# Row 0 of a two-layer graph kernel, loaded as two halves of 512 columns instead of pairs of whole blocks

## The chip, the cores and the metric

The kernel runs on one NeuronCore of one Trainium2 chip. A core has five engines that work side by side, each with its own queue of instructions: TensorE (PE in the profile; its weight loads are shown as PEld) multiplies matrices into PSUM, VectorE (DVE) and ScalarE (ACT) work element by element, GpSimd (POOL) does small things here, and SyncE (SP) issues the loads and stores, which 16 DMA engines carry out. An engine takes its instructions in the order in which the program wrote them; semaphores make it wait for another engine or for a load. The metric is the device time of one execution in microseconds (us).

## The reference

Inputs are x (4096 nodes x 64 features), a 4096 x 4096 matrix adj of float32 that is mostly zeros, and small weights. Cut to what matters:

```python
h = relu(layernorm(x))
x1 = tanh(concat([adj @ h, h]) @ W[0])        # hop 0
x2 = tanh(concat([adj @ x1, x1]) @ W[1])      # hop 1
x = x + x2
h = relu(layernorm(x))
support = h @ weight
mask = adj != 0
rank = cumsum(mask, axis=1); deg = rank[:, -1:]
k = minimum(deg, 100); pos = rank - (deg - k)
w = mask * where(pos > 0, 0.5 ** (k - pos), 0)
out = x + w @ support + bias
```

So adj is needed as numbers twice, since hop 1 cannot start before hop 0 has given x1, and once as counts: the weight of an entry depends on how many nonzero entries follow it in its row.

## The kernel before

**Tiling.** adj is taken transposed, in blocks of 128 source nodes (on the partitions, the axis that a matmul sums over) by 1024 destination nodes. There are four rows of destinations (I = 0 to 3) and 32 blocks in each (b = 0 to 31); a block is 512 KB. A chunk of eight blocks has the same 1024 nodes as a row, so blocks 0 to 7 are row 0's own nodes. The matrix is 64 MB and doesn't fit into SBUF.

**Two sweeps.** sweep1 (L418) reads all of adj once, in units of two blocks (1 MB), 16 a row, from block 31 down to block 0. Each unit gets hop 0 on TensorE (agg_pair, L266: two matmuls of 64 output rows, one for each half of 512 columns, side by side in the two column groups of the array) and count_pair (L248) on VectorE: nonzero entries are marked (L254, or for some units on ScalarE, mark_on_act, L240), the mark and the running count are stored as one byte an entry in `code` (L261), and the count goes on (L262). Where x1 of a block is known already (b < 8 I), hop 0 and hop 1 are done in one matmul of 128 rows (L483). sweep2 (L811) loads again the blocks for which hop 1 is missing (72, by its plan at L816, row 0's blocks 8 to 31 last), does their hop 1 and, between these, layer 1 with weights that ScalarE and VectorE make out of `code` (L690, L682, L685); its order is planned by a cost model when the program is built (clock, use, decode).

**What sets the order in sweep1.** The loop over units (L447) writes the instructions of all engines, unit by unit: loads up to k + 5 (load, L426), norms, counting, matmuls, then one step of whatever generator stands in `steps`. A loaded unit goes into a place (places, L106): five of a ring, or parts of `code` that are not yet written. A place is free when its former unit has been counted and multiplied; SP waits for that when it issues the load, and all later loads stand behind it.

**The norms.** ln_relu (L184) takes up to eight blocks in three steps (sum and centre, sum of squares, scale), with ScalarE squaring (L193) and GpSimd taking the power (L197). Before unit 0, VectorE norms blocks 30 and 31, then 24 to 29, then 16 to 23; the chunks 8 to 15 and 0 to 7 follow at units 2 and 5. features_T (L285) transposes a chunk on TensorE, own_share (L227) multiplies it with W.

**The end of row 0.** When row 0 is summed, finish_row(0) (L350) runs as steps between the first units of row 1: the sums go to SBUF (L364), x1 is made (L210, L223), transposed and multiplied with W[1] (L336) and copied out (L348). Then hop 1 of row 0's own eight blocks is done from the last four units of row 0, which are held in their places until then:

```python
            own = [v for k in sorted(held) for v in held[k]]
            for n, (b, a) in enumerate(own):
                agg_pair(acc[0][:, 0, :], at(b)[:, D:], a, n == 0, n == len(own) - 1)
            held.clear()
```

After it L390 adds its product, totals (L298) and count_after (L303) turn the row's counts into what follows each entry, and set_after (L310) stores that; settle (L408) later subtracts it from `code`.

Of the kernel before, what the change touches and what calls it, by code (L numbers as in the profile page):

```python
# [44 lines left out]
def gnn_kernel(  # L45
# [61 lines left out]
    for J in range(NCH):  # L107
        for j in range(NB // CB):
            v = code[J][j].rearrange("p b i -> p (b i)").bitcast(F32)
            v = v.rearrange("p (s i) -> p s i", i=CW)  # L110
            places.append([v, J * NB // 2 + (NB - CB * (j + 1)) // 2, -1])

    cnts = [cnt[:, i].rearrange("p h i -> p (h i)") for i in range(2)]
# [35 lines left out]
    def load_weights():  # L149
        nc.sync.dma_start(wb, weights)  # L150
        for h in range(2):
            rows = slice(h * D, (h + 1) * D)
            nc.gpsimd.tensor_copy(
                wz[rows, h], wb[rows, : HOPS * 2].rearrange("p (k a) e -> p k a e", a=2)
            )
        nc.gpsimd.tensor_copy(xw[:D, 1, :], wb[:D, 3, :])
        nc.gpsimd.tensor_copy(xw[D:, 1, :], wb[D:, 2, :])
# [48 lines left out]
    def paired(po, terms, first=True, last=True):  # L206

        for n, (w, v) in enumerate(terms):
            for c in range(NC):
                nc.tensor.matmul(  # L210
                    po[c * D : (c + 1) * D, :], w(c), v(c),
                    start=first and n == 0, stop=last and n == len(terms) - 1,
                )

    def x1_of(po, I, terms, xs, at_=None):


        paired(po, terms, at_ is not None)
        if at_ is not None:
            nc.vector.tensor_tensor(at_, po, flat(pre1[:, chunk(I), :]), op=ALU.add)  # L220
            po = at_
        for c in range(NC):
            nc.scalar.activation(xs[c][:D], po[c * D : (c + 1) * D, :], AF.Tanh)  # L223

    own0 = []

    def own_share(I):  # L227

        h = flat(pre1[:, chunk(I), :])
        po = two(name="po") if I else one(name="po")  # L230
        paired(po, [(lambda c: wz[:, c, 0, 1], lambda c: h)], last=I > 0)
        if I:
            nc.scalar.copy(h, po)
        else:
            own0.append(po)
# [3 lines left out]

    def mark_on_act(I, b, a):  # L240


        m = codes_at(I, b)
        sign = m.bitcast(I8)
        nc.scalar.activation(sign, a, AF.Sign)  # L245
        nc.scalar.activation(m, sign, AF.Square, scale=float((FLAG - 1 + 0.25) ** 0.5))  # L246

    def count_pair(I, b, a, marked):  # L248

        cnt = cnts[I % 2]  # L250
        q = codes_at(I, b)
        m = q if marked else mbuf[:, b // 2 % 2]
        if not marked:
            nc.vector.tensor_scalar(  # L254
                m, a, 0.0, float(FLAG - 1), op0=ALU.not_equal, op1=ALU.mult
            )
        q, m = (v.rearrange("p h i -> p (h i)").bitcast(U16) for v in (q, m))
        if b == NB - 1:
            nc.vector.tensor_scalar(q, m, float(FULL * 257), None, op0=ALU.add)
        else:  # L260
            nc.vector.tensor_tensor(q, m, cnt, op=ALU.add)  # L261
        nc.vector.tensor_scalar(cnt, q, 0x7F7F, None, op0=ALU.bitwise_and)  # L262

# [39 lines left out]
    def count_after(I, tot, acc):  # L303

        banks = [acc[0][:, c, :] for c in range(NC)] if I else [acc[1], acc[0][:, 1, :]]
# [20 lines left out]

    def x1_and_share(I, xs):
# [3 lines left out]
        K_ = P if I else D  # L331
        for h, pt in enumerate(banks):
            pt = pt.rearrange("p (t w c e) -> p t w c e", t=2, w=2, c=NC)
            for t in range(2):
                for c in range(NC):
                    nc.tensor.matmul(  # L336
                        pt[:, t, :, c, :], by_t(xs[c])[:K_, h, t, :], xw[:K_],
# [4 lines left out]
    def halves_of(banks, w):  # L342
        for h, pt in enumerate(banks):
            yield h, pt.rearrange("p (t w c e) -> p t w c e", t=2, w=2, c=NC)[:, :, w]

    def take(dst, banks, w):
        for h, pt in halves_of(banks, w):
            nc.scalar.copy(as_nodes(dst)[:, 2 * h : 2 * h + 2], pt)  # L348

    def finish_row(I, acc, held):  # L350
        if I:

            T = [tmp(name="T") for _ in range(NC)]
            for c in range(NC):
                nc.scalar.copy(T[c][:D], acc[0][:D, c, :])
                nc.scalar.copy(T[c][D:], acc[1][c * D : (c + 1) * D])
            xs = [tmp(name="x1T") for _ in range(NC)]
            for c in range(NC):
                nc.scalar.copy(xs[c][D:], acc[0][D:, c, :])
            terms = [(lambda c: w0, lambda c: T[c])]  # L360
        else:
            xs = [tmp(name="x1T") for _ in range(NC)]
            S = tmp(name="S")
            nc.scalar.copy(S, acc[1])  # L364
            terms = [(lambda c: wz[:, c, 0, 0], lambda c: S)]
        both = tmp([P, CW], U8, name="both")
        yield
        x1_of(one(name="po") if I else own0.pop(), I, terms, xs, T[1] if I else None)
# [3 lines left out]
        if I:  # L372
            yield
        banks = x1_and_share(I, xs)
        counts = count_after(I, tot, acc)
        take(hxs[I][:, :, D:], banks, 0)
        if I == 0:
            yield

            own = [v for k in sorted(held) for v in held[k]]  # L380
            for n, (b, a) in enumerate(own):
                agg_pair(acc[0][:, 0, :], at(b)[:, D:], a, n == 0, n == len(own) - 1)
            held.clear()
            G = tmp(name="G")
            nc.scalar.copy(G, acc[0][:, 0, :])
            yield
            g = by_t(G)
            for h, pt in halves_of(banks, 1):
                for t in range(2):
                    nc.tensor.matmul(  # L390
                        pt[:, t], g[:, h, t, :], wz[:, :, 1, 0, :],
                        start=False, stop=True, skip_group_check=True,
                    )
# [23 lines left out]

    def sweep1():  # L418
        b0 = NB - 2
        load_x(NCH - 1)  # L420
        first = ln_relu(hxs[-1][:, CB - 2 :, :D], pre1[:, b0:, :])
        pairs = [(I, b) for I in range(NCH) for b in range(NB - 1, 0, -2)]
        tiles = []
        held = {}

        def load(upto, done):  # L426

            while len(tiles) < min(upto, len(pairs)):
                k = len(tiles)
                I, b = pairs[k]  # L430
                free = [v for v in places if k + MARGIN <= v[1] and v[2] < done and v[2] not in held]
                if not free:
                    assert k > done
                    return
                place = min(free, key=lambda v: v[2])
                place[2] = k
                a = place[0]
                n = NB - 1 - b
# [8 lines left out]
        for k, (I, b) in enumerate(pairs):  # L447
            n = k % (NB // 2)
            if n == 0:
                acc = sums_of("acc")  # L450
            if k == 0:
                load(1, 0)
                load_x(2)
                load(2, 0)
                load_x(1)
                load(3, 0)
                load_x(0)
            if k == 6:
                load_weights()
            load(k + 5, k)  # L460
            if k == 0:
                next(first)
                next(first)
                rest = ln_relu(hxs[-1][:, : CB - 2, :D], pre1[:, NB - CB : b0, :])
                next(rest)
                for _ in first:
                    pass
                next(rest)
                more = ln_relu(hxs[2][:, :, :D], pre1[:, chunk(2), :])
                for _ in rest:  # L470
                    pass
                next(more)
                steps.append(more)
            if k in (2, 5):
                q = 1 - k // 3
                steps.append(ln_relu(hxs[q][:, :, :D], pre1[:, chunk(q), :]))
            a = tiles[k]
            count_pair(I, b, a, k in marked)
            for r in (1, 0):
# [9 lines left out]
                if I == 0 and g < CB:  # L489
                    held.setdefault(k, []).append((g, a[:, r]))  # L490
            step()
            if k in (4, 6, 9, 13):
                features_T({4: 3, 6: 2, 9: 1, 13: 0}[k])
            if k in (10, 12, 14, 15):
                own_share({10: 3, 12: 2, 14: 1, 15: 0}[k])

            j = k + (2 if k < NB // 2 - 2 else 3)
            if j < len(tiles):
                m = j % (NB // 2)
                if m % 2 == 1 and m >= 3 if j < NB // 2 else m % 3 == 2 and m > 3:  # L500
                    mark_on_act(*pairs[j], tiles[j])
                    marked.add(j)
            if I > 1 and n % 2 == 1:
                settle()
            if n == NB // 2 - 1 and I < NCH - 1:
                steps.append(finish_row(I, acc, held))
# [5 lines left out]

# [7 lines left out]
    def finish_last(acc):  # L520
# [13 lines left out]
        x1_of(one(name="po"), I, [(lambda c: w0, lambda c: T[c])], xs, T[1])  # L534
# [3 lines left out]
        counts = count_after(I, tot, acc)  # L538
# [272 lines left out]
    def sweep2(acc):  # L811
# [14 lines left out]
        def load(k, r, a, t):  # L826
            I, b = blocks[len(tiles)]
            nc.sync.dma_start(a, adjA[I, NB - 2 - b // 2 * 2 + b % 2])
# [132 lines left out]
```

## Time and profile before

| what | us |
|---|---|
| median of three runs | 348.49 (347.23 to 349.1) |
| the profiled execution | 349.98 |
| its span, first to last instruction | 347.3 |
| TensorE busy | 328.1 (94%) |
| VectorE busy | 274.0 (79%) |
| ScalarE busy | 199.9 (58%) |
| read from HBM | 107.15 MB, 312 GB/s over the span |

The profile's times count from the first instruction. A line of the chain of waits has a start, a length and what was late; a line of the timeline has start, length, engine, source line, operation, the tiles written and read, and in brackets how long the engine had been idle and what ended that. A matmul in float32 of 512 columns shows as two records, and the records of the two column groups overlap, so a block of hop 0 is four records. The row numbers L... are lines of the kernel before.

### The profile page before, as it was taken

To read this page: it belongs to the slowest core of one execution; us is meant where nothing else is said; L and a number is where in the kernel's file an instruction comes from. 1 tells how busy PE (TensorE), PEld (TensorE's weight loads), DVE (VectorE), ACT (ScalarE), POOL (GpSimd) and SP (SyncE) were. 2 spreads that over 40 slices of the span, in tenths; PEclk is the share of its full clock that TensorE was granted. 3 is DMA by queue.
4 is the path that set the end of the run, shared out by engine and by line. 5 is a ranking of instruction groups with operands and counts; after the bars stand their busy time and mean duration, and the time that the engine had idled before them with its cause. 6 is when DMAs were issued, how large, how long until landed. Compare 5 with 4: busy or idle time off the path is not lost.

```text
span 347.3 us, 3829 instructions
## 1 busy us (share of the span) xinstructions
PE 328.1 (94%) x1356; PEld 154.7 (45%) x1360; DVE 274.0 (79%) x402; ACT 199.9 (58%) x204; POOL 24.6 (7%) x22
## 2 busy tenths in 40 slices
PE   2787899999999999999999999999999999998995
PEld 0133344333434344344444343243444656467785
DVE  4988688779749999999999585878256799989953
ACT  2087885184447453266043344136458989979980
POOL 2320200000000000000000000412003000003000
PEclk9999999999999999999999999999999999999999
DMA  7999999999999999884989799999998937400012
GB/s 241 413 410 406 410 408 408 411 408 408 411 408 408 406 366 390 286 321 143 416 291 346 287 401 380 355 413 410 408 408 304 356 112 249 166 0 0 3 44 76
DMA packets 30466, 108.44 MB, mean 312 GB/s; under 512 B 2416, under 2 KB 3824, under 8 KB 30448
## 3 DMA queue, kind: packets, MB, share of 16 engines
q1 hardware_dynamic: 30448, 108.21, 81.0%
q8 instruction: 10, 0.16, 0.2%
q14 instruction: 8, 0.07, 0.0%
HBM read 107.15 MB, written 1.05 MB: 312 GB/s over the span
## 4 chain that ended last, share of the span: by engine, by line
PE 73%; DMA 18%; ACT 3%; issue 2%; DVE 2%; SPq 1%; ACTq 0%; DVEq 0%
PE acc L483 24%; PE acc L268 17%; PE accl L750 12%; PE acc_low L268 12%; DMA codes<-in_adjA_dram 11%; DMA ring<-in_adjA_dram 7%; PE pt L336 2%; PE pto L798 2%; ACT weights L690 2%; PE po L210 2%; PE py L577 1%; DVE weights L685 1%; ACT codes L245 1%; DVE bits L682 0%; PE pt L390 0%
## 5 line engine op out<-in xcount | busy, mean ns | idle before, releaser
L690 ACT ACTIVATE weights<-codes 128x1024 fp32r<-128x1024 uint8 x90 | 86.7, 1044 | 12.7 <-PE accl L750 9.8
L483 PE MATMUL acc<-ring,hx 128*128 128x512 f32 x176 | 76.5, 594 | 0.0
L268 PE MATMUL acc<-ring,hx 128*64 128x512 f32 x288 | 66.9, 599 | 0.8 <-DMA ring<-in_adjA_dram 0.7
L750 PE MATMUL accl<-weights,feat 128*128 128x512 f32 x254 | 63.5, 400 | 1.3 <-DVE feat L624 1.0
L750 PEld LDWEIGHTS accl<-weights,feat 128*128 128x128 f32 x254 | 46.0, 188 | 21.2 <-ACT weights L690 7.3
L483 PEld LDWEIGHTS acc<-ring,hx 128*128 128x128 f32 x176 | 33.2, 190 | 43.1 <-issue 43.1
L268 PE MATMUL acc_low<-codes,hx 128*64 128x512 f32 x192 | 45.7, 595 | 3.6 <-DMA codes<-in_adjA_dram 3.4
L268 PE MATMUL acc_low<-ring,hx 128*64 128x512 f32 x128 | 34.7, 660 | 9.3 <-DVE hx L200 6.3
L412 DVE TENSOR_TENSOR codes<-codes,after 128x2048 uint16<-128x2048 uint16 x32 | 38.3, 1220 | 0.1
L268 PEld LDWEIGHTS acc<-ring,hx 128*64 128x64 f32 x288 | 19.2, 136 | 40.0 <-issue 31.9
L246 ACT ACTIVATE codes<-codes 128x2048 uint8<-128x2048 int8 x19 | 36.3, 1910 | 0.6
L254 DVE TENSOR_SCALAR mbuf<-ring 128x2048 uint8<-128x2048 f32 x30 | 36.6, 1220 | 0.0
L245 ACT ACTIVATE codes<-ring 128x2048 int8<-128x2048 f32 x8 | 15.3, 1914 | 30.1 <-DMA ring<-in_adjA_dram 26.3
L685 DVE TENSOR_SCALAR weights<-bits 128x1024 fp32r<-128x1024 f32 x37 | 26.6, 719 | 7.1 <-PE accl L750 3.7
L261 DVE TENSOR_TENSOR codes<-mbuf,cnt 128x1024 uint16<-128x1024 uint16 x41 | 28.4, 692 | 1.5
L262 DVE TENSOR_SCALAR cnt<-codes 128x1024 uint16<-128x1024 uint16 x64 | 27.5, 429 | 2.2
L268 PEld LDWEIGHTS acc_low<-codes,hx 128*64 128x64 f32 x192 | 14.2, 136 | 29.2 <-issue 20.3
L245 ACT ACTIVATE codes<-codes 128x2048 int8<-128x2048 f32 x11 | 21.0, 1913 | 10.0 <-DMA codes<-in_adjA_dram 10.0
L682 DVE TENSOR_SCALAR bits<-codes 128x1024 uint32<-128x1024 uint8 x37 | 25.6, 691 | 0.8
L598 POOL TENSOR_TENSOR pre<-pre,wb 128x512 f32<-128x512 f32 x4 | 5.5, 1379 | 262.9 <-DVE xc L192 262.9
L268 PEld LDWEIGHTS acc_low<-ring,hx 128*64 128x64 f32 x128 | 9.6, 148 | 29.8 <-issue 13.9
L261 DVE TENSOR_TENSOR codes<-codes,cnt 128x1024 uint16<-128x1024 uint16 x19 | 13.1, 690 | 8.4 <-ACT codes L246 7.6
(89 smaller groups left out, 239.0 us busy)
## 6 DMA issues: line engine op xcount, KB each, us to landing
ring<-in_adjA_dram SPq DMA_DIRECT2D x74, 512.0 KB, 6.6
ring<-in_adjA_dram SPq DMA_DIRECT2D x37, 1024.0 KB, 8.4
codes<-in_adjA_dram SPq DMA_DIRECT2D x26, 1024.0 KB, 18.2
pre<-in_x_dram SPq DMA_DIRECT2D x4, 256.0 KB, 7.5
xres<-in_x_dram SPq DMA_DIRECT2D x4, 256.0 KB, 6.6
out_dram<-o SPq DMA_DIRECT2D x3, 256.0 KB, 2.6
out_dram<-o SPq DMA_DIRECT2D x2, 128.0 KB, 2.2
wb<-in_weights_dram SPq DMA_DIRECT2D x1, 192.0 KB, 17.5
```

Source lines behind the costliest of these rows:

```text
L245: nc.scalar.activation(sign, a, AF.Sign)
L246: nc.scalar.activation(m, sign, AF.Square, scale=float((FLAG - 1 + 0.25) ** 0.5))
L254: nc.vector.tensor_scalar(m, a, 0.0, float(FLAG - 1), op0=ALU.not_equal, op1=ALU.mult)
L261: nc.vector.tensor_tensor(q, m, cnt, op=ALU.add)
L262: nc.vector.tensor_scalar(cnt, q, 0x7F7F, None, op0=ALU.bitwise_and)
L268: nc.tensor.matmul(acc[c * D : (c + 1) * D, :], src, a[:, c * C : (c + 1) * C], start=first, stop=last,)
L412: nc.vector.tensor_tensor(q, q, a[:, None, :].to_broadcast([P, 4, CW // 2]), op=ALU.subtract)
L483: nc.tensor.matmul(acc[0][:, c, :], at(g), a[:, r, c * C : (c + 1) * C], start=g == CB * I - 1, stop=g == 0,)
L682: nc.vector.tensor_scalar(state["bits"], q, float(ZERO), ONE, op0=ALU.subtract, op1=ALU.mult)
L685: nc.vector.tensor_scalar(w, state["bits"].bitcast(F32), 2.0 ** (127 - LOW), None, op0=ALU.mult)
L690: nc.scalar.activation(w, q, AF.Exp, scale=LN2, bias=BIAS)
L750: nc.tensor.matmul(sums[g][:, c, :], feats[J][:, k, :], w[:, c * C : (c + 1) * C], start=first, stop=last,)
```

## The change

Row 0 alone is treated in another way; rows 1 to 3 and sweep2 keep their loops.

- A unit of row 0 is now four blocks by 512 columns, again 1 MB: first the eight units of columns 0 to 511 (blocks 31 down to 0), then those of columns 512 to 1023, of which the unit with blocks 0 to 3 is loaded first. The host lays row 0 out for this, so that a unit is as contiguous as before. The even and the odd block of a pair go to the two column groups of TensorE and are added by the next matmul. sweep2 fetches a block of row 0 as two runs of 2 KB a partition where it was one of 4 KB.
- When the first half is summed (unit 7), x1 of its 512 nodes, which are blocks 0 to 3, is made in steps beside the second half, and hop 1 of these four blocks follows at units 10 to 13, one block at a time. The second half's x1 and hop 1 of blocks 4 to 7 come between the first units of row 1. Units 6, 7, 8 and 15 stay in their places until hop 1 has read them.
- Counting follows the blocks from the end, so it runs in half-size steps (two blocks by 512 columns each), starts two units late, and counts unit 8 last, after unit 15. The units that ScalarE marks in row 0 are 3, 5, 7, 11, 13, 15 (before, 9 as well).
- The first norm takes four blocks, the next four, and the chunk 16 to 23 is split in two; all norms are written by unit 2. Loads are issued up to k + 6; the weights are loaded at unit 1 instead of 6, and the copies made of them are spread over units 1, 4 and 5.
- The parts of `code` of chunk 0 are no longer among the places.

The diff, cut to its core:

```diff
-    for J in range(NCH):
+    for J in range(1, NCH):
...
+    def marks_at(I, b):
         if I:
+            return codes_at(I, b)
+        c, q = b
+        return code[0][q // 2][:, q % 2 * 4 : q % 2 * 4 + 4, c * C : (c + 1) * C]
...
+    def count_step(q, m, cnt, first):
+        q, m = q.bitcast(U16), m.bitcast(U16)
+        if first:
             nc.vector.tensor_scalar(q, m, float(FULL * 257), None, op0=ALU.add)
         else:
             nc.vector.tensor_tensor(q, m, cnt, op=ALU.add)
         nc.vector.tensor_scalar(cnt, q, 0x7F7F, None, op0=ALU.bitwise_and)
...
+        c, n = b
+        for r in (2, 0):
+            count_step(
+                q[:, r : r + 2], m[:, r : r + 2], cnt[:, 0, :, c * (C // 2) : (c + 1) * (C // 2)],
+                n == NB // 4 - 1 and r == 2,
+            )
...
+    def finish_first(acc, quads):
+
+        low, G, po, banks = acc
+        xs = {}
+
+        def x1_half(c):
+            S = tmp(name="S")
+            nc.scalar.copy(S, low[c])
+            yield
+            nc.tensor.matmul(po[c * D : (c + 1) * D], w0, S, start=False, stop=True)
+            xs[c] = tmp(name="x1T")
+            nc.scalar.activation(xs[c][:D], po[c * D : (c + 1) * D], AF.Tanh)
+            yield
+            for h in range(2):
+                pt = nodes(banks[h])
+                for t in range(2):
+                    nc.tensor.matmul(
+                        pt[:, t, :, c, :], by_t(xs[c])[:D, h, t, :], xw[:D],
+                        start=t == 0 and c == 0, stop=True, skip_group_check=True,
+                    )
+            for h in range(2):
+                nc.scalar.copy(
+                    as_nodes(hxs[0][:, :, D:])[:, 2 * h : 2 * h + 2, c], nodes(banks[h])[:, :, 0, c]
+                )
+
+        def hop1(b):
             for c in range(NC):
+                nc.tensor.matmul(
+                    G[c * D : (c + 1) * D, :], at(b)[:, D:], part_of(quads[c, b // 4], b),
+                    start=b == 3, stop=b == 4,
+                )
+
+        yield from x1_half(0)
+        for b in range(3, -1, -1):
+            yield
+            hop1(b)
+        busy.difference_update(k for k in (7, 8))
+        yield "next"
         both = tmp([P, CW], U8, name="both")
+        yield from x1_half(1)
+        yield
+        for b in range(7, 3, -1):
+            hop1(b)
+        busy.difference_update((6, 15))
...
+        marks0 = {1: 3, 3: 5, 7: 7, 9: 11, 11: 13, 13: 15}
+        to_count = [*range(8), *range(9, 16), 8]
+
+        for k in range(2 * NQ):
+            _, (c, q) = units[k]
...
+            if k == 1:
+                copies = load_weights()
+            if k in (1, 4, 5):
+                next(copies, None)
+            load(k + 6)
...
+                for g in (first, first, rest, first, rest, ends[0], rest, ends[0], ends[1], ends[0], ends[1]):
+                    next(g, None)
+                lns[2] = ends[1]
+            a = tiles[k]
+            if c == 0 or q < 2:
+                quads[c, q] = a
+            for b in (4 * q + n for n in (2, 3, 0, 1)):
+                h = b % 2
+                nc.tensor.matmul(
+                    low0[c][h * D : (h + 1) * D, :], at(b)[:, :D], part_of(a, b),
+                    start=b >= NB - 2 if c == 0 else k == 8 and b > 1,
+                    stop=b < 2 if c == 0 else k == 15 and b < 6,
+                )
+            order_ = {
+                0: (1, 1, 2), 1: (0, 1, 0), 2: ("n", 0),
+            }.get(k, ("n", "n") if k == 7 else ("n",))
...
+            if k == 7:
+                own_share(0, po0)
+                steps.append(finish_first((low0, sums0[:, 0, :], po0, banks0), quads))
+            if k >= 7 and steps:
+                if next(steps[0]) == "next":
+                    state0.append(steps.pop(0))
+            if k in (1, 4, 5, 6):
+                features_T({1: 3, 4: 2, 5: 1, 6: 0}[k])
+            if k in (7, 8, 10):
+                own_share({7: 3, 8: 2, 10: 1}[k])
+            if k in marks0:
+                mark(marks0[k])
...
-            nc.sync.dma_start(a, adjA[I, NB - 2 - b // 2 * 2 + b % 2])
+            if I:
+                nc.sync.dma_start(a, adjA[I, NB - 2 - b // 2 * 2 + b % 2])
+            else:
+                v = adjA[0].rearrange("(c j) p (h i) -> j h p c i", c=NC, h=2)[b // 2, b % 2]
+                nc.sync.dma_start(a.rearrange("p (c i) -> p c i", c=NC), v)
```

## The prediction

> **What bounds the kernel now.** I read the page first, then the chain of waits, then one table by stage, and last the timeline of the places where the chain changes hands. The page's own summary of the chain says that TensorE is late most of the time and DMA second:
>
> ```profile
> PE 73%; DMA 18%; ACT 3%; issue 2%; DVE 2%; SPq 1%; ACTq 0%; DVEq 0%
> ```
>
> The chain in order of time (start, length, what) tells where each of the two is late:
>
> ```profile
> 11.78 19.38 DMA codes<-in_adjA_dram
> ...
> 31.17 18.26 DMA codes<-in_adjA_dram
> ...
> 54.32 1.08 PE po L210 x4
> ...
> 61.60 6.87 PE acc L268 x32
> ...
> 71.33 13.88 PE acc_low L268 x64
> 85.21 13.93 PE acc L483 x32
> ```
>
> Row 0 is a stream of loads up to 49.4 us; from 54.3 on it is TensorE without a break up to 218 us. The 6.87 us are hop 1 of row 0's eight own blocks (32 records, 0.86 us a block): the work of which the change moves half. The 13.88 us are eight units (0.435 x 4 = 1.735 us each); L483 is the fused part of row 1. The table by stage (us, then busy PE, PEld, DVE, ACT, POOL, clock, DMA share, GB/s) shows that two resources are full at once:
>
> ```profile
> 6.30:49.40 43.10, 36.93 (x196) 13.23 (x196) 34.08 (x55) 27.90 (x22) 9.25 (x8) 1.00 1.02 408
> 49.40:85.10 35.70, 35.38 (x173) 13.22 (x170) 29.04 (x43) 20.14 (x18) 0.00 (x0) 1.00 1.03 409
> 85.10:99.10 14.00, 14.00 (x36) 6.03 (x34) 10.64 (x16) 3.82 (x2) 0.00 (x0) 1.00 1.03 411
> 99.10:197.80 98.70, 98.41 (x301) 42.55 (x304) 89.50 (x119) 45.21 (x44) 0.00 (x0) 1.00 0.89 338
> ```
>
> In row 0 TensorE has some 6 us idle, so work moved there can hide. But in row 1 the DMA engines run at 409 to 411 GB/s as well. How far TensorE lags behind the loads there is the number that decides. ScalarE shows it, because it marks unit 27 and unit 30 as soon as they land (the bracket: it sat idle until a load came), beside TensorE's first fused weights (unit 28):
>
> ```profile
> 80.59 1.91 ACT L245 ACTIVATE codes<-codes 128x2048 int8<-128x2048 f32 x1 [3.39 <-DMA codes<-in_adjA_dram]
> 85.14 0.30 PEld L483 LDWEIGHTS acc<-ring,hx 128*128 128x128 f32 x2 [0.81 <-issue]
> 88.27 1.91 ACT L245 ACTIVATE codes<-ring 128x2048 int8<-128x2048 f32 x1 [3.83 <-DMA ring<-in_adjA_dram]
> ```
>
> A unit lands every (88.27 - 80.59) / 3 = 2.56 us, so unit 28 lands at 83.15 and TensorE takes it up at 85.14: **a lead of 2.0 us**. It is the smallest of the row (units 29 and 30: 2.9 and 3.9, since fused units cost 3.48 us). TensorE may gain as much as it likes before unit 28; only 2.0 us can pass it.
>
> **The change part by part.**
>
> *TensorE, row 0.* Hop 0 keeps its count: 4 matmuls a unit, still alternating between the two column halves, 1.735 us. From the landing of unit 7 (27.7 in the trace, + 0.5 since the 192 KB of weights now go ahead of it: 28.2) TensorE must do units 7 to 15 (9 x 1.735 = 15.6), four own_share (4 x 0.86 = 3.4), x1 of one half (one matmul alone, 0.43 to 0.86, I take 0.86; half of the 2.08 of L336, 1.04) and hop 1 of four blocks (3.44). ScalarE adds a wait: the tanh of the first half stands behind the marking of unit 7 (about 3.85 us from 32.5), so the transposes start near 37.1 instead of 36.7: 0.4. Sum 24.8 us, so unit 15 is done at 53.0, against 51.4 before. The idle time took most of it, and TensorE is some 2.0 us behind unit 15's landing.
>
> *TensorE, row 1 up to unit 28.* From 49.46 (unit 15's landing): lag 2.0; units 15 to 27 13 x 1.735 = 22.6; x1 of the second half 0.86 + 1.04; hop 1 of the other four blocks 3.44; L390 1.14; counts 0.5; and 0.4 of waiting for the totals (below). Sum 32.0: TensorE is ready at 81.4 for a unit that lands at 83.15. The saving so far is 3.7 us; 2.0 pass, and 1.7 turn into waits for loads at units 25 to 28. I take 1.9, because the first weights after such a wait are not overlapped (0.1).
>
> *After unit 28* nothing absorbs it that I can find. Unit 40 lands at 113.8 and is taken up at 117.35: a lead of 3.5, 1.6 are left. From 121 us the loads are issued as places come free, so they move with the engines. VectorE is near full in rows 2 and 3 but is released by TensorE (5.02 us idle before L220 at 102.70, 0.73 at 148.58). The loads of hop 1 after 184 us wait for TensorE (69.3 us of SP's waits are L828 on it), so the DMA-bound 218 to 237 us move too. Places are handed out to the same units in the same order as before, so no load of rows 1 to 3 gets another slot.
>
> *Norms.* The first takes four blocks instead of two: reduce, centre, square, reduce, pow, scale grow from 0.29, 0.29, 0.31, 0.29, 0.70, 0.29 towards the six-block rows (0.55 and 1.33); the first matmul moves from 6.34 to about 7.1. It costs nothing, since TensorE waits for unit 1 (10.99) anyway. All 32 blocks must now be normed by unit 6 (25.7) instead of unit 12; adding VectorE's rows in the new order I get blocks 20-23 at 11.1 (needed 14.2), 16-19 at 14.9 (17.5), 8-15 at 17.7 (20.0), 0-7 at 22.0. Without that 2.3 us of cover TensorE would start units 4 to 6 late, still ahead of row 1's slack.
>
> *Counting.* It is done in half-size steps, twice as many:
>
> ```profile
> L261 DVE TENSOR_TENSOR codes<-mbuf,cnt 128x1024 uint16<-128x1024 uint16 x12 | 8.3, 692 | 0.5
> ...
> L322 DVE TENSOR_TENSOR after<-after 128x512 uint16<-128x512 uint16 x1 | 0.4, 424 | 0.0
> ...
> L319 DVE TENSOR_SCALAR after<-cnt 128x512 uint16<-128x512 uint16 x1 | 0.3, 282 | 0.0
> ```
>
> Start to start a pair of half steps is 0.46 + 0.32 (113.39, 113.07 us), so a unit costs 1.56 instead of 1.07: + 0.5 x 16 = 7.8 us, and unit 9 is no longer marked by ScalarE (+ 1.22). Norms 12.8, ten unmarked units of 2.8, six marked of 1.56 and the waits: the last, unit 8, which is counted after unit 15 (marked at 53.3), has its values read by 56.1 and is done at 57.7. Who waits: the load of unit 21, which goes into unit 8's place, with every later load queued behind it on SP. An unqueued 1 MB load takes 4.7 us to land:
>
> ```profile
> DMA to landing us min/median/max: 4.7/16.2/20.7
> ```
>
> It has to land at 65.1, so it may be issued as late as 60.4: 4 us of cover. The row's totals come after counts 16 to 18 (65.1, and 66.2 with ScalarE's cast): the 0.4 of wait above. Bounds: 0 if VectorE catches up, 9 if none of its growth were hidden.
>
> The Trainium skill (VectorE: DVE Perf Modes, The TRN2 errata) speaks against splitting: a fixed cost of about 58 cycles, 60 ns, per instruction, to be spread by tiles of 512 elements or more. By it the two extra instructions of a unit cost an estimated 0.12 us, 1.9 in the row; the rows above make it 7.8, and they decide.
>
> *Row 0's reload for hop 1* comes in runs of 2 KB instead of 4. In the trace's packets the 1,024 of 2 KB (x) take a median 84 ns, the 25,600 of 4 KB 159 ns: 16 x 84 against 8 x 159 per engine, + 0.07 us a load, 24 x 0.07 = 1.7 at most. Those loads land 3.7 us or more ahead of their matmuls, the last one (303.9 for 305.3) 1.4 ahead: I take 0, with 1.7 as the other end. The Trainium skill (DMA: Bandwidth & Descriptors, Specifications) puts line rate at 512 B and up, which would make this 0 by itself; the packets say 6%.
>
> *Smaller copies, earlier weights, a look-ahead of 6*: ScalarE's three extra copies stand beside loads; the load queue is full either way. 0.
>
> **Sum.** -1.9 us. The profiled execution took 349.98 us (span 347.3) and would take 348.1; it lies 1.5 above the median of 348.49. On that median: **346.6 us**.
>
> **The rivals.**
> 1. *The forecast*, 346.0 to 347.2: chance 0.58. For it: the lead of 2.0 is measured, and TensorE has 1.7 us to spare at it.
> 2. *The work moved does not fit beside the second half*, 347.2 to 349.5, near 348.5: chance 0.19. ScalarE's 3.85 us markings stand ahead of the tanh and the copies that TensorE needs. One more such wait in full costs 3.85 - 1.7 = 2.1, the whole gain. Against it: I find only 0.4.
> 3. *VectorE holds the loads*, slower: chance 0.15. Should half steps cost what whole ones do (0.72 + 0.35 each), a unit grows by 1.07 instead of 0.5: 9 us more, unit 8 is read at 65, unit 21 lands 4.7 later at 69.7 instead of 65.1, and the full DMA stream is 4.6 late at unit 28: 4.6 - 2.0 = + 2.6, 351.1. It decides from a release at 62.4 on. Against it: the 512-element rows do cost less.
> 4. *The stream itself lands earlier*, 344.5 to 346: chance 0.08. Two gaps between landings (3.45 us at unit 8, 2.93 at unit 19, against 2.56) are worth 1.3 if they don't recur; that would give 345.3.
>
> Rival 3 lies outside the range on its upper side, and half of 4 below: 345.0 to 349.6. A measurement here tells 0.5% (1.74 us) from no change, and my forecast lies just over it, at 346.75: of case 1 two thirds count as faster, 0.39; with case 4, 0.47. The same: 0.36 (a third of 1, most of 2). Slower: 0.17.
>
> **What would show it.** Right: hop 1's L268-type records of acc split in two groups of 16, one inside 38 to 51 us; TensorE waiting for DMA at units 25 to 28; the first fused weights near 83.2 and the same distance from there to the end. Wrong: TensorE without waits up to unit 28 (rival 2), an SP wait on VectorE and a hole in GB/s near 60 to 70 us (rival 3), or waits that the 2 KB loads cause near 300.

## The result, and the profile after

The changed kernel takes **346.25 us** (median of 7 runs, 345.14 to 346.92) against 348.13 for the kernel before (7 runs, 347.23 to 349.13): a ratio of 0.994, with a 95% interval of 0.9919 to 0.996. That is 1.9 us less (1.4 to 2.8 by the interval), as forecast. Its profiled execution took 346.92 us, with a span of 345.1 (before: 349.98 and 347.3). Each is the longest of its kernel: the seven runs of the changed kernel span 343.4 to 345.1 us. So times are compared by ratios, and traces of single executions tell only where time goes. In a later group of runs the changed kernel took 346.5 us against 348.22, a ratio of 0.9954 (0.9939 to 0.9969).

The summary of the chain of waits on the page of the changed kernel. TensorE's share has fallen from 73% to 65%, and those of VectorE (2% before) and ScalarE (3% before) have grown:

```profile
PE 65%; DMA 17%; DVE 7%; ACT 5%; issue 2%; SPq 1%; ACTq 0%; DVEq 0%
```

The chain itself (start, length, what), from the end of row 0's counts on:

```profile
64.43 0.34 DVE both L312
...
64.87 18.11 DMA ring<-in_adjA_dram
82.98 0.14 issue
83.11 13.97 PE acc L593 x32
97.08 1.87 PE acc_low L280 x8
...
115.29 27.66 PE acc L593 x64
```

Unit 28, the first fused one (L593, formerly L483), begins at 83.11 instead of 85.14. But it is now a load that releases it: landed at 82.98, first in use at 83.11. The chain goes back from this load to its issue and so comes to VectorE, which had freed its place. But the load was in the queue for 18.11 us behind others that land 2.56 us apart, so VectorE's larger share is no sign that VectorE held it up. From unit 28 to the end of the span are 262.0 us (345.1 - 83.1), and before they were 262.1 (347.3 - 85.2). So the difference in these two traces arises before unit 28, and nothing clear of the scatter is gained or lost after it (the same distance is 261.0 to 261.8 us in after_again, hop1_together, reload_4k and norms_undone below). The later unbroken stretch (27.66 us from unit 40) starts 2.06 earlier too, and its load has landed only 1.56 ahead of it (113.73).

TensorE's timeline in the changed kernel (start, length, line, operation, tiles; in brackets the idle time and what ended it):

```profile
39.85 1.03 PE L385 MATMUL acc<-codes,hx 128*64 128x512 f32 x4
...
43.29 1.03 PE L385 MATMUL acc<-codes,hx 128*64 128x512 f32 x4
...
45.86 1.03 PE L385 MATMUL acc<-codes,hx 128*64 128x512 f32 x4
...
48.44 1.03 PE L385 MATMUL acc<-codes,hx 128*64 128x512 f32 x4
49.29 3.60 PE L545 MATMUL acc<-codes,hx 128*64 128x512 f32 x16
...
60.02 3.60 PE L385 MATMUL acc<-codes,hx 128*64 128x512 f32 x16
...
68.61 8.75 PE L280 MATMUL acc_low<-codes,hx 128*64 128x512 f32 x40
77.90 1.94 PE L280 MATMUL acc_low<-codes,hx 128*64 128x512 f32 x8 [0.53 <-DMA codes<-in_adjA_dram]
80.46 1.94 PE L280 MATMUL acc_low<-codes,hx 128*64 128x512 f32 x8 [0.63 <-DMA codes<-in_adjA_dram]
83.11 2.38 PE L593 MATMUL acc<-ring,hx 128*128 128x512 f32 x5 [0.71 <-DMA ring<-in_adjA_dram]
```

L385 is hop 1 of row 0's own blocks: four of them, 0.86 us each, now stand between units of the second half, and the other four follow in row 1. The stretch of units 21 to 27 (56 records) begins at 68.61; before it began at 73.02. So TensorE has **saved 4.4 us** by then. Three brackets tell what becomes of it: units 26, 27 and 28 wait for loads, 0.53 + 0.63 + 0.71 = 1.87 us, and by the lengths another 0.5 goes as TensorE starts again after each wait. 4.4 - 2.4 = 2.0 comes through.

The table by stage of the changed kernel (us, then busy PE, PEld, DVE, ACT, POOL, clock, DMA share, GB/s), cut at the places that answer to the first two stages before (unit 15's landing, unit 28's start):

```profile
6.30:49.50 43.20, 40.16 (x220) 16.16 (x222) 37.58 (x83) 26.57 (x26) 9.10 (x10) 1.00 1.02 406
49.50:83.10 33.60, 31.74 (x148) 11.10 (x145) 31.46 (x52) 17.66 (x16) 0.00 (x0) 1.00 1.03 409
```

In row 0 TensorE is busy for 40.16 us where it was 36.93, in the same 43 us: the moved work fills its idle time. In row 1 it now idles 33.60 - 31.74 = 1.86 us, while the DMA engines run at the same 409 GB/s. The granted clock is 1.00 in all of it, before and after.

### The profile page after: what moved, and what is told of

It reads as the page before. It is cut to its first block, busy times and chain, and to the rows that moved or that the text cites. A ratio compares the mean times of both kernels' runs of the same rounds, so it can differ in the third digit from the quotient of the medians.

```text
span 345.1 us, 3882 instructions
## 1 busy us (share of the span) xinstructions
PE 327.8 (95%) x1360; PEld 155.8 (45%) x1360; DVE 280.9 (81%) x440; ACT 197.1 (57%) x206; POOL 24.6 (7%) x23
## 4 chain that ended last, share of the span: by engine, by line
PE 65%; DMA 17%; DVE 7%; ACT 5%; issue 2%; SPq 1%; ACTq 0%; DVEq 0%
PE acc L593 24%; PE acc L280 17%; PE accl L851 12%; DMA ring<-in_adjA_dram 11%; PE acc_low L280 6%; DMA codes<-in_adjA_dram 6%; PE pto L899 2%; ACT weights L791 2%; PE pt L348 2%; ACT codes L246 2%; ACT codes L245 2%; DVE codes L253 1%; PE po L211 1%; DVE mbuf L261 1%; DVE weights L786 1%
## 5 line engine op out<-in xcount | busy, mean ns | idle before, releaser
L593 PE MATMUL acc<-ring,hx 128*128 128x512 f32 x176 | 76.5, 594 | 0.7 <-DMA ring<-in_adjA_dram 0.7
L280 PE MATMUL acc<-ring,hx 128*64 128x512 f32 x288 | 66.7, 598 | 0.9 <-DMA ring<-in_adjA_dram 0.9
L593 PEld LDWEIGHTS acc<-ring,hx 128*128 128x128 f32 x176 | 33.2, 190 | 43.8 <-issue 42.3
L280 PEld LDWEIGHTS acc<-ring,hx 128*64 128x64 f32 x288 | 19.4, 136 | 39.7 <-issue 32.7
L246 ACT ACTIVATE codes<-codes 128x2048 uint8<-128x2048 int8 x18 | 34.4, 1910 | 0.6
L254 DVE TENSOR_SCALAR cnt<-codes 128x1024 uint16<-128x1024 uint16 (+1 forms) x80 | 30.0, 375 | 2.7
L253 DVE TENSOR_TENSOR codes<-mbuf,cnt 128x1024 uint16<-128x1024 uint16 (+1 forms) x51 | 30.6, 600 | 1.8
L245 ACT ACTIVATE codes<-codes 128x2048 int8<-128x2048 f32 x10 | 19.1, 1913 | 13.4 <-DMA codes<-in_adjA_dram 10.7
L280 PE MATMUL acc_low<-codes,hx 128*64 128x512 f32 x104 | 25.1, 595 | 1.2 <-DMA codes<-in_adjA_dram 1.2
L280 PE MATMUL acc_low<-ring,hx 128*64 128x512 f32 x88 | 22.1, 598 | 0.0
L545 PE MATMUL acc_low<-ring,hx 128*64 128x512 f32 x40 | 11.7, 715 | 9.0 <-DVE hx L201 7.0
L261 DVE TENSOR_SCALAR mbuf<-codes 128x2048 uint8<-128x2048 f32 x16 | 19.5, 1220 | 0.0
L198 POOL TENSOR_TENSOR s<-s,half 128x8 f32<-128x8 f32 (+1 forms) x10 | 16.9, 1692 | 15.8 <-DVE s L197 15.8
```

Source lines behind the costliest of these rows:

```text
L245: nc.scalar.activation(sign, tile_of(I, a), AF.Sign)
L261: nc.vector.tensor_scalar(m, tile_of(I, a), 0.0, float(FLAG - 1), op0=ALU.not_equal, op1=ALU.mult)
L280: nc.tensor.matmul(acc[c * D : (c + 1) * D, :], src, a[:, c * C : (c + 1) * C], start=first, stop=last,)
L593: nc.tensor.matmul(acc[0][:, c, :], at(g), a[:, r, c * C : (c + 1) * C], start=g == CB * I - 1, stop=g == 0,)
```

## The experiments

Twelve runs follow, of ten further kernels, one of them twice, and of the changed kernel again (after_again), in three groups, each on one chip with runs of the kernel before in between. A ratio is against those runs; in brackets its 95% interval. The theory is the one on record: a saving ahead of unit 28 counts only up to that unit's lead, because the load stream is full. Line numbers move by a few between the kernels; L483, L589, L592, L593, L594 and L596 are all the fused matmul, L268 and L280 hop 0 or hop 1 of one pair.

**1. Work taken away from TensorE in the kernel before** (before_less_hop1): hop 1 of seven of the eight own blocks of row 0 is left out.

```diff
-            own = [v for k in sorted(held) for v in held[k]]
+            own = [v for k in sorted(held) for v in held[k]][:1]
```

> The kernel before with hop 1 of only one of row 0's eight own blocks (seven left out, 6.0 us of matmuls). Theory: only the 2.0 us by which TensorE is behind the loads at unit 28 can be gained; 4 us become waits for loads; unit 28 near 83.1, span 345.3. Rival (TensorE is the bound throughout): all 6.0 us, span 341.3.

Measured: 0.9934 (0.992 to 0.9947), 2.3 us less, although 6.0 us of matmuls are gone. TensorE's timeline in this kernel:

```profile
80.26 1.94 PE L268 MATMUL acc_low<-codes,hx 128*64 128x512 f32 x8 [0.62 <-DMA codes<-in_adjA_dram]
82.82 7.56 PE L483 MATMUL acc<-ring,hx 128*128 128x512 f32 x17 [0.62 <-DMA ring<-in_adjA_dram]
```

Unit 28 begins at 82.82, 2.3 earlier, and units 24 to 28 wait 0.5 to 0.6 us each. The cap is real and belongs to the kernel before, not to the change.

**2 and 3. The cap lifted** (after_less_load, before_less_load): the load of unit 20 is left out in either kernel, so that every later load of the stream is one unit ahead; unit 20's matmuls read what lies in the place.

```diff
-                else:
+                elif k != 20:
                     (the load)
```

> The changed kernel without the load of unit 20 (its place keeps the values of unit 4, so the output is wrong from there on); all else stays. Theory: every later unit lands 2.56 us sooner, TensorE's waits at units 26 to 28 (1.9 us) go, unit 28 is taken up near 81.2 and the span falls by 1.9 to 343.2. Rival (TensorE's work sets the gain, the waits are incidental): no change, 345.1.

> The kernel before without the load of unit 20 (its place keeps the values of unit 4, so the output is wrong from there on). Theory: TensorE is 2.0 us behind the loads at unit 28 there, so loads that land sooner change nothing before it: span 347.3, within 0.5. Rival (the loads of row 1 hold both kernels): 2 us faster.

Measured: on the changed kernel 0.9892 (0.9877 to 0.9907), that is 344.34 us, with no wait in row 1 and unit 28 at 81.05; on the kernel before 1.0005 (0.9991 to 1.0019), unit 28 at 84.83. The chains of waits, of after_less_load and, last, of before_less_load:

```profile
67.16 13.88 PE acc_low L280 x64
81.05 13.93 PE acc L593 x32
...
84.83 13.93 PE acc L483 x32
```

The same load less is worth some 2 us where TensorE waits for the stream and nothing where it lags. With 1 this pins the bound on both sides: before, TensorE is late at unit 28 by about 2 us; after, the loads are, by about as much.

**4. The headline move undone** (hop1_together): hop 1 of all eight own blocks is done together in row 1 again; everything else stays.

```diff
         yield from x1_half(0)
-        for b in range(3, -1, -1):
-            yield
-            hop1(b)
-        busy.difference_update(k for k in (7, 8))
...
-        for b in range(7, 3, -1):
+        for b in (3, 2, 1, 0, 7, 6, 5, 4):
             hop1(b)
-        busy.difference_update((6, 15))
+        busy.difference_update((6, 7, 8, 15))
```

> The changed kernel with one part undone: hop 1 of blocks 0 to 3 is no longer made beside the second half, but together with blocks 4 to 7 between the first units of row 1 (3.44 us of matmuls move back). Theory (the loads up to unit 28 set the gain): unit 15 is then taken up at its landing, 1.5 us sooner, and TensorE uses up its waits of 0.53 + 0.63 + 0.71 = 1.9 us at units 26 to 28; 3.44 - 1.5 - 1.9 = 0, so unit 28 is still taken up near 83.1 and the span stays at 345.1, within 0.5. Rival (the gain is the matmul time moved into row 0): the gain of 2 us is lost, span 347.

Measured: 0.9961 (0.9947 to 0.9975), against 0.994 and 0.9954 for the changed kernel. The chain of waits of this kernel:

```profile
69.82 13.88 PE acc_low L280 x64
83.70 13.93 PE acc L589 x32
```

No break: TensorE is late again, at 83.70, 1.07 us after unit 28 has landed (82.63). So moving hop 1 has brought about 0.6 us of the 2.0 at unit 28 by these two traces; by the ratios it is 0.2 to 0.7 us. (This trace's span, 344.7, is below the changed kernel's 345.1, but it makes up 1.2 us between 214 and 226 us, where the changed kernel's chain has 7.17 us of waiting for loads from 216.29 on; up to there it is behind.) The other 1.5 (85.2 to 83.7) has come from the rest of what the halves allow. About 0.2 of it is there when row 1 begins: own_share's last product is made at 39.8 instead of 51.4, and unit 16 starts at its landing, at 52.02 instead of 52.25. Most of the rest lies in x1, of which only one half now stands behind the row (its transposes take 1.21 us instead of 2.15). Neither was tried alone.

**5. VectorE made late** (late_release): unit 8 is counted after units 16 to 18, so its place comes free later.

```diff
-        for j in to_count:
-            counted(j)
-            busy.discard(j) if j not in (6, 7, 8, 15) else None
...
-            load(k + 5)
+            if k > 18:
+                load(k + 5)
...
+            if k == 18:
+                counted(8)
+                load(k + 5)
```

> The changed kernel with one thing moved: VectorE counts unit 8 not after unit 15 but after units 16, 17 and 18, so that it lets go of its place three counts (7.0 us) later, and the load of unit 21 and all behind it are issued near 63.2 instead of 56.2; no work is added, TensorE's order stays. Theory: an unqueued load takes 4.7 us, so unit 21 lands at 67.9 instead of 65.1; the stream is 2.8 us late from there, unit 28 lands at 85.8 and all of it reaches the end: span 347.9, the gain gone. The 4 us of cover that the prediction counted are used up first. Rival (TensorE's backlog absorbs it, 68.6 is when it takes up unit 21): span 345.1 to 346.

Measured: 1.0071 (1.005 to 1.0093), 350.46 us; the span of 348.9 is 3.8 above that of the changed kernel, 1 us more than expected (the six runs span 347.5 to 349.3). TensorE's timeline in this kernel:

```profile
72.78 1.94 PE L280 MATMUL acc_low<-codes,hx 128*64 128x512 f32 x8 [0.62 <-DMA codes<-in_adjA_dram]
...
81.89 5.35 PE L280 MATMUL acc_low<-codes,hx 128*64 128x512 f32 x16 [2.06 <-DMA codes<-in_adjA_dram]
87.17 3.27 PE L594 MATMUL acc<-ring,hx 128*128 128x512 f32 x7
```

Unit 8 is read by 62.67, unit 21's load is issued at 62.73 and lands at 67.62, 2.5 us later than in the changed kernel (65.08): that much is rival 3, with its place and its price. The bracket of 2.06 is another 1.4: unit 26 lands 3.99 us after unit 25 instead of 2.56. An instruction fetch of 1.15 us stands on one DMA engine just then (78.87), but whether it makes the gap was not tried.

**6. The reload in runs of 4 KB** (reload_4k): hop 1 reads row 0's blocks again in one run a partition, with values that belong to other nodes.

```diff
-                v = adjA[0].rearrange("(c j) p (h i) -> j h p c i", c=NC, h=2)[b // 2, b % 2]
-                nc.sync.dma_start(a.rearrange("p (c i) -> p c i", c=NC), v)
+                nc.sync.dma_start(a, adjA[0, b])
```

> The changed kernel with row 0's reload for hop 1 in runs of 4 KB a partition instead of 2 KB (it then reads other values of the row, so hop 1 of row 0 is wrong); count and size of the loads stay. Theory: these loads land 1.4 us or more ahead of their matmuls, so it is worth nothing: span 345.1, within 0.3. Rival (the 2 KB runs cost up to 0.07 us a load and the last stage waits for them): up to 1.7 us faster.

Measured: 0.9945 (0.9927 to 0.9963). The first five of these loads land 1.28 us apart where the 2 KB runs need 1.35, the 0.07 worked out, and nothing waits for them: from unit 28 to the end it is 261.8 us, against 262.0. The span of this trace is 343.8, 1.3 below the 345.1 expected, which looks like the rival. But 1.1 of it is there at unit 28, long before any reload: the stream landed earlier in this execution. TensorE's timeline in this kernel:

```profile
81.99 13.97 PE L593 MATMUL acc<-ring,hx 128*128 128x512 f32 x32 [0.71 <-DMA ring<-in_adjA_dram]
```

The ratio lies between the two of the changed kernel (0.994, 0.9954), so it shows no gain either.

**7. The finer norms undone** (norms_undone): two blocks first, then six, then whole chunks of eight.

```diff
-        b0 = NB - CB // 2
-        first = ln_relu(hxs[-1][:, CB // 2 :, :D], pre1[:, b0:, :])
+        b0 = NB - 2
+        first = ln_relu(hxs[-1][:, CB - 2 :, :D], pre1[:, b0:, :])
...
-                for g in (first, first, rest, first, rest, ends[0], rest, ends[0], ends[1], ends[0], ends[1]):
+                for g in (first, first, rest, first, rest, rest, lns[2], lns[2]):
...
```

> The changed kernel with the old split of the norms (two blocks, six, then eight for blocks 16 to 23). Theory: unit 0 starts at 6.3 as before the change; blocks 16 to 23 are normed near 16.5 and unit 2, which landed at 13.7, waits 3 us for them, but TensorE catches up at 1.735 us a unit against 2.56 us a load before the second half; span 345.1 to 345.6. Rival (the finer norms are where the gain is): 2 us slower, 347.

Measured: 0.9945 (0.9933 to 0.9958). The first matmul starts at 6.25 instead of 7.02, but unit 0's second half waits until 9.39 and unit 2 begins at 14.88. Unit 28 still waits for its load (82.40); the span of 343.9 is below the 345.1 to 345.6 expected, again because the stream landed earlier. The split neither costs nor brings anything here: either order is ready before the stream lets row 1 use it. I had reckoned with some 17 us for unit 2.

**8 and 9. The waits filled** (fused_early, and again as fused_early_again): the same units, bytes and matmuls, but in row 1 the fused units, which cost TensorE 3.48 us instead of 1.735, are put between the others, where TensorE now waits. Counts keep their order.

```diff
-        units += [(I, b) for I in range(1, NCH) for b in range(NB - 1, 0, -2)]
+        units += [(1, b) for b in (*range(NB - 1, 13, -2), 7, 13, 5, 11, 9, 3, 1)]
+        units += [(I, b) for I in range(2, NCH) for b in range(NB - 1, 0, -2)]
+        later = {25: (), 27: (), 29: (29, 25), 30: (27, 30)}
...
-            counted(k)
+            for j in later.get(k, (k,)):
+                counted(j)
...
```

> The changed kernel with row 1 in another order: the units with blocks 7, 6 and 5, 4 (fused, 3.48 us of matmuls each) are loaded and multiplied as the tenth and twelfth of the row instead of the thirteenth and fourteenth, and are counted in their old order, from places that are held until then. Same work, same bytes. Theory: TensorE's waits at units 26 to 28 (1.9 us) are filled, since a fused unit takes longer than the 2.56 us of a load; row 1 ends 1.5 to 1.9 sooner, and the next limit is unit 40, where 1.56 us of lead are left: span 343.6. Rival (the order of units makes no difference, the bound is TensorE's work): 345.1.

> fused_early as it was, beside the changed kernel on one chip. Theory: 1.2 to 2 us below it, ratio to before 0.989 to 0.992. Rival (no difference, what was seen is scatter): the same ratio as the changed kernel.

> The changed kernel as it is, to stand beside fused_early on one chip: span 345.1, ratio to before 0.994.

Measured: 345.08 us, 0.992 (0.9906 to 0.9934); again, beside the changed kernel on one chip: 345.14, 0.9918 (0.9898 to 0.9939), where the changed kernel had 0.9954 (0.9939 to 0.9969). On that one chip it is 0.36% faster than the changed kernel, about 1.3 us by the ratios. TensorE's timeline in fused_early:

```profile
75.74 3.70 PE L596 MATMUL acc<-codes,hx 128*128 128x512 f32 x8
79.37 1.94 PE L280 MATMUL acc_low<-codes,hx 128*64 128x512 f32 x8
81.24 3.70 PE L596 MATMUL acc<-codes,hx 128*128 128x512 f32 x8
...
95.52 1.94 PE L280 MATMUL acc_low<-ring,hx 128*64 128x512 f32 x8
```

No bracket is left, and row 2 begins at 95.52 instead of 97.0. It is 1.5 and not 2.4 because unit 20 began 0.17 later here (67.01 against 66.84) and, above all, because the row itself has become longer: its units 20 to 31 take 28.51 us in a row (67.08 to 95.59), where hop1_together, without waits too, needs 27.81 (69.82 to 97.63). That is 0.70 us for four more changes between matmuls of 64 and of 128 output rows, 0.17 each. The Trainium skill (TensorEngine Tiling (Array Packing), Key Properties) says that changing the tiling mode drains TensorE and gives no price; the trace fits that, as it shows time lost at these changes, and has the price. Of the lead at unit 40 only 0.28 is left in this trace (landed at 113.52, taken up at 113.80): the next saving ahead of it would be capped there.

**10 and 11. Where the move pays** (fused_early_hop1_together, before_fused_early): the new order with hop 1 undone as in 4, and the new order on the kernel before.

```diff
# before_fused_early
+        pairs = [(0, b) for b in range(NB - 1, 0, -2)]
+        pairs += [(1, b) for b in (*range(NB - 1, 13, -2), 7, 13, 5, 11, 9, 3, 1)]
...
-            count_pair(I, b, a, k in marked)
+            for j in later.get(k, (k,)):
+                count_pair(*pairs[j], tiles[j], j in marked)
...
```

> Both edits at once: row 1 in the order of fused_early, and hop 1 of row 0's eight blocks made together between the first units of row 1. Theory: with hop 1 together TensorE has no wait for loads in row 1 that the new order could fill (it took up unit 28 at 83.70, landed at 82.63), so this stays where hop1_together was, span 344.7 to 345.0; undoing the move of hop 1 then costs 1.7 to 2.0 us in this order, against about 0.6 in the old one. Rival (the move of hop 1 is worth the same few tenths everywhere): 343.4 to 343.6.

> The kernel before with row 1 in the order of fused_early. Theory: TensorE is 2.0 us behind the loads at unit 28 there and waits for none, so the order fills nothing: span 347.3, within 0.5. Rival (the order is good by itself): 1.5 to 2 us faster, 345.5.

Measured: 347.88 us, 0.9997 (0.9983 to 1.0011), with a span of 346.4 where I had expected 344.7 to 345.0; and 348.49, 1.0007 (0.9994 to 1.002), no change, as expected. Set out as ratios to the kernel before:

| | order of before | fused units early |
|---|---|---|
| kernel before | 1 | 1.0007 |
| changed, hop 1 together | 0.9961 | 0.9997 |
| changed | 0.994, 0.9954 | 0.992, 0.9918 |

The chain of waits of fused_early_hop1_together:

```profile
60.53 6.87 PE acc L385 x32
...
70.69 8.73 PE acc_low L280 x40
79.42 3.63 PE acc L592 x8
...
99.20 1.87 PE acc_low L280 x8
```

With hop 1 in one piece (6.87 us), TensorE never waits for the stream in row 1 after unit 16 and runs without a break to the end of the row, at 99.20. The new order has no wait to fill there, as expected, and its 0.70 to pay (70.69 to 99.20 is 28.51 again), which my expectation had left out. On the kernel before the same stretch grows by the same 0.70 (28.51 for 27.81), though the ratio does not show it beyond its interval. The order is a gain only where loads are last. Read by columns, the table says where the headline move pays: 0.2 to 0.7 us in the order of before, less than the width of a ratio's interval, but 0.9997 - 0.9918 = 0.0079, or 2.75 us (1.9 to 3.6 with both intervals; 1.7 to 2.0 expected), with the fused units early, most of the 3.44 of matmuls moved. By the ratios hop1_together loses 1.25 us by the new order, where the changes between 64 and 128 rows make 0.70; with both intervals that is some 0.6 to 1.9, so nothing more than the 0.70 is shown. In the profiled execution its whole stream also lands 0.9 us later (unit 16: 52.84 against 51.98). That difference is there at unit 9 (34.92 against 34.06), up to which the two kernels do the same, so it is the scatter of the stream between executions and not the new order.

## Why the prediction was right

**The cap at unit 28** was the step that carried the forecast, and it held: 83.11 for a forecast near 83.2, 1.87 us of waits for 1.7, and the same 262 us from there to the end. That it holds to a tenth is luck, though: unit 28 begins at 83.34 in after_again, 82.40 in norms_undone and 81.99 in reload_4k, each time released by its load, and the spans follow (344.9, 343.9, 343.8). The stream's landing moves by more than 1 us from one execution to the next, and the end moves with it, which is the cap once more. Summing instructions alone would have given -3.7 or more; experiment 1 shows 6.0 us removed and 2.3 gained.

**TensorE's own saving** was somewhat larger than worked out: 4.4 instead of 3.7 at the start of units 21 to 27. The sum itself carried a lag of 2.0 us at unit 15 where its own numbers give 53.0 - 1.735 - 49.46 = 1.8. The 0.4 of wait for the totals did not occur: the totals were cast at 65.84 and used at 66.32, behind L410. In the first half, x1's matmuls run beside those of own_share in the other column group (33.4 to 34.3) and cost about half of the 0.86. Unit 15 was done at 52.7 (53.0), and the transposes of the first half began at 36.95 (37.1). Since the loads cap it, the extra 0.7 became waits and changed nothing. Also, I had put 0.1 on restarting TensorE after a wait; it is 0.5 for three.

**VectorE's growth stayed hidden.** Its timeline in the changed kernel, at the half steps and at unit 8:

```profile
45.97 0.43 DVE L253 TENSOR_TENSOR codes<-mbuf,cnt 128x512 uint16<-128x512 uint16 x1
46.43 0.29 DVE L254 TENSOR_SCALAR cnt<-codes 128x512 uint16<-128x512 uint16 x1
46.76 0.43 DVE L253 TENSOR_TENSOR codes<-mbuf,cnt 128x512 uint16<-128x512 uint16 x1
...
54.94 1.22 DVE L261 TENSOR_SCALAR mbuf<-codes 128x2048 uint8<-128x2048 f32 x1
```

A pair of half steps takes 46.76 - 45.97 = 0.79, so a unit 1.58 (1.56 worked out). Unit 8 is read by 56.16 (56.1); unit 21's load is issued at 56.22 and lands at 65.08 (65.1), in a stream that is full anyway. SyncE does wait 9.7 us on VectorE for that place, which the prediction named as a sign of rival 3; but the other sign, a hole in the stream, is missing (units 20 to 22 land at 62.52, 65.08 and 67.63). The rows of the trace for 512 elements had the right price; the estimate by the Trainium skill's fixed cost of 58 cycles (VectorE: DVE Perf Modes, The TRN2 errata), 0.12 us a unit, would have been too small by four. The same section remarks that its row is too low and that about 150 cycles were measured (some 155 ns, if 58 are 60), which the rows here bear out: 2 x 424 - 692 = 156 ns of fixed time in a TENSOR_TENSOR. Rival 3 did not come about, but late_release shows that its 4 us of cover are all there were.

**The norms** came at 11.7, 15.5, 17.7 and 21.9 (11.1, 14.9, 17.7, 22.0), the first matmul at 7.02 (7.1), and experiment 7 confirms the zero. **The reload** at +0.07 a load, and worth nothing, is confirmed by 6. **Unit 40's lead** is 1.56 (1.6).

**What the prediction did not say** is which part of the change earns the 1.9 us. It priced hop 1's 3.44 us in one sum with the rest; by experiment 4 the change without that move would already have had most of it. Rival 2 (work that doesn't fit) is refuted: ScalarE's marking of unit 7 delays the tanh to 35.82, and TensorE has other work meanwhile. Rival 4 did not come about in this profile: the gap at unit 8's landing is there again, 3.9 us (3.45 before), unit 19's is gone (2.57 for 2.93), but unit 6 now lands 3.08 us after unit 5, and unit 28 lands at 82.98. In reload_4k, with the same loads up to there, the stream did come 1.1 us earlier, so single executions can meet rival 4's condition.

## What to carry to other kernels

Before adding up what an edit saves, look for the places where the engine meets a full stream of transfers, and read its smallest lead there: nothing saved ahead of it passes beyond that. Read it in more than one trace: here the landings moved by over 1 us between executions. An engine that waits for the same landings (ScalarE here) shows them where the late engine hides them. Once the cap is reached, a change of order that puts long work where the waits are is worth more than further savings; the same change of order only makes the row longer where there is no wait to fill (0.70 us here), so measure the two together.

## What was not expected of the hardware

- TensorE loses about 0.17 us at each change between matmuls of 64 and of 128 output rows (0.70 for four), and about as much when it starts again after a wait for a load (0.5 for three).
- Runs of 2 KB are 5 to 6% slower than runs of 4 KB in a full stream (1.35 against 1.28 us for 512 KB), though the Trainium skill (DMA: Bandwidth & Descriptors, Specifications) lets line rate begin at 512 B.
- The stream has gaps that no instruction of an engine explains: 3.9 us at unit 8 in the changed kernel, 3.99 at unit 26 in late_release, for 2.56. Each time a fetch of instructions, 16 KB and 1.1 us long, lies on one of the 16 DMA engines; but a like fetch at 76.3 us in the changed kernel made no gap, so the cause is open.
